# Handing the early expert jobs over to the late ones: two transposes ahead of outputs, one row load on another queue, scatters in a row, and the last gates in two halves

## Chip, cores and metric

The kernel runs on one core of one Trainium2 chip. The metric is the time on the device in microseconds (us) of one execution. A profiled execution is one more run, recorded by the hardware profiler; its span is the recorded stretch inside that execution.

## What is computed

The reference takes `x` of 8 x 512 tokens of width 256 and a context of 8 x 64 tokens, all float32, and does four steps in a row, each added to `x`:

```python
x = x + cross_attention_0(layernorm(x), ctx)          # 16 heads of 16
x = x + top_k_ffn(layernorm(x))                       # gelu on 384 of 512 tokens of each batch
x = x + cross_attention_1(layernorm(x), ctx, mask)
x = x + moe(layernorm(x))                             # 8 experts, top 2, inner width 1024

def moe(h):                                           # h: 4096 tokens x 256
    probs = softmax(h @ gate_w.T); w, idx = top_k(probs, 2); w = w / sum(w)
    for each expert e:
        g, u = split(h @ gate_up[e].T)
        out += combine[:, e] * ((silu(g) * u) @ down[e].T)
```

The last step is the larger half of the time. Here it is computed sparsely: each token goes through its two experts only.

## The kernel before, in words

**Front part.** For each batch a chain of steps does the two attentions, the first feed-forward, and then the routing (`route_steps`): the gate, the choice of two experts, and eight row scatters (`sent_off`, L864) on GpSimd (POOL), which write each token's normalised row, with its number and its two weights behind it, into the DRAM table `xs`, sorted by expert. The chains of the eight batches are interleaved by a string written out by hand, `ORDER`: a digit or letter stands for the next step of one chain, and `in_order` ties the instructions of every compute engine to that order. The last scatters of batch 7 are the last `7`s of the string. A scatter is also held until the matrix product that stands before it in the string is done (`products`).

**Early jobs.** A job is 256 rows of `xs` for one expert. Seven jobs (`NEARLY`) run inside the front part, chain `j`, on rows of batches 0 to 3. Each has: `load` (row number and expert from `jobs_early`, then the rows into `e_xg`), four `load_piece` and `load_down` (weights, on SyncE's queue), `enter` (four transposes `ps_e`, a copy to `e_xT` on ScalarE, and five small VectorE operations for token numbers and weights), four steps `gates(n)` of two chunks each (`gate_up`: four matmuls, a tanh on ScalarE, two VectorE operations, into `e_hT`), and two steps `down(k)` (eight matmuls, the weighted product `e_now` on VectorE, and an indirect DMA on POOL that adds the rows to the output, `add_rows`, L106). There is a single set of weights, `e_wgu` and `e_wdn`, and a single `e_sg`, so the tanh of a chunk waits until VectorE is done with the chunk before. PSUM tiles of this part come from `ps_m`, four buffers in turn.

**Lists.** `early_list` and `full_list` (chain `l`) work out on VectorE which expert and rows each job has. `full_list` stands behind job 6's `enter` in `ORDER`; it writes `jobs` and `job_e` for the late full jobs. `small_list` and `unit_list` are traced later and fill VectorE's gaps beside job 6's gates.

**Late jobs.** 18 full jobs of 256 rows (`NLATE`), seven of 128 rows and ten or eleven pairs of up to 64 rows run after the front part, in the list `order`; the last in it is a full job. Each has `load` (row numbers, rows into `xg`, weights into one of four sets, all on SyncE's queue), `enter` (transposes `ps_x`, copy to `xjT`), gates (`gate_up_full` or `gate_up_rows`) and `down`. The loop runs `down` of a job behind the gates of the next one. The first late job is special: its `load` was called with `late=True`, which puts its row load behind its gate weights, and its `enter` follows the last `down` of the early jobs. Row loads wait for `routed`, the scatters of batch 7. `unit_list` also writes rows of zeros behind each expert's rows (L1080, L1082, on POOL), after the row loads of the first two late jobs have landed; the pairs' row loads wait for that.

What `down` sends must wait for the adds of the job before it, since two jobs may hold the same token:

```python
ahead[:] = sent          # the adds of the job before
sent.clear()
...
sent.append(add_rows(now, tok[:, k : k + 1]))
```

Of the kernel before, what the change touches and what calls it, by code (L numbers as in the profile page):

```python
# [8 lines left out]
F32 = mybir.dt.float32  # L9
I32 = mybir.dt.int32  # L10
AF = mybir.ActivationFunctionType
ALU = mybir.AluOpType
# [3 lines left out]
P = 128  # L16
# [3 lines left out]
D = 256  # L20
H = 16
DK = 16
NC = D // P
# [4 lines left out]
E = 8  # L28
TOPK = 2
FF = 1024  # L30
NF = FF // P
# [3 lines left out]
QROWS = B * S + P  # L35
RW = D + 4
NFULL = 25
NEARLY = 7
NLATE = NFULL - NEARLY
# [15 lines left out]
5264345645256352452222F36F35F63F222246455635547335546357453674356647435356733333556646v7  # L55
l63333476G464jj77j5jGj666j5j7jj47Gjjj765j7457j4G5j64654j7j6556747j5j7644644444j76sH6jj56
4444j557j76j7j57jj7Hsj76jjjjHH7565j65jj676jj7jj6j57j5j6j75557j5555jj7j6j667j55557jjjs67j
66j76j7676j66j76s66667j7jjjj7jj6666j77j7j7jjjjj77jjs7j7j7j7j7j777jj77jjjljj77jj77jj
"""


# [1 line left out]
def xattn_ffn_kernel(ctx: ExitStack, tc: tile.TileContext, a: dict, out: bass.AP):  # L63
    nc = tc.nc
# [52 lines left out]
    with ExitStack() as front:  # L117
        const = front.enter_context(tc.tile_pool(name="const", bufs=1))
        work = front.enter_context(tc.tile_pool(name="work", bufs=2))
        small = front.enter_context(tc.tile_pool(name="small", bufs=4))  # L120
# [986 lines left out]
        e_xg = part_of_room(2, RW)  # L1107
        e_xT = part_of_room(NC, 2, P)
        e_sg = [part_of_room(1, 2 * P)]
        e_now = keep.tile([P, 2, D], F32, name="e_now")  # L1110
        e_w = {}
        piece = 2 * P

# [128 lines left out]
        chains["j"] = early = []  # L1242
        jobs_steps = [early_steps(j) for j in range(NEARLY)]
        early += jobs_steps[0][0]
        for j, (_, steps) in enumerate(jobs_steps):

            loads = list(jobs_steps[j + 1][0]) if j + 1 < NEARLY else []
            for n, step in enumerate(steps):
                early.append(step)
                if loads and n != len(steps) - 2:  # L1250
                    early.append(loads.pop(0))


        engines = (
# [46 lines left out]
    def kind(j):  # L1301
        return "full" if j < NLATE else "one" if j < NLATE + NONE else "pair"

    def load(j, late=False):

        what = kind(j)
        subs, n = (2 if what == "full" else 1), (2 if what == "pair" else 1)
        first = j if what != "pair" else NLATE + NONE + 2 * (j - NLATE - NONE)
        size = P if what != "pair" else P // 2

        with tc.issue_after(last.pop().ins) if last else nullcontext():
            at = [
                (
                    nc.sync.value_load(
                        jobs[0:1, 0, u : u + 1], min_val=0, max_val=E * QROWS + P - subs * size
                    ),
                    nc.sync.value_load(jobs[0:1, 1, u : u + 1], min_val=0, max_val=E - 1),
                )
                for u in range(first, first + n)
            ]  # L1320
        xg = moe.tile([P, 2, RW], F32, tag="xg", name=f"xg_{j}", bufs=3)

        def rows():
            for u, (row, _) in enumerate(at):
                i = nc.sync.dma_start(
                    xg[u * size : u * size + size, 0:subs, :],
                    xs[bass.ds(row, subs * size), :].rearrange("(s p) w -> p s w", p=size),
                ).ins

                if what == "pair":  # L1330
                    after(i, tail_sent)
                else:
                    for other in tail_sent:
                        tc.declare_no_dep(i, other, reason="rows of tokens alone")
                    after(i, routed)

        if not late:
            rows()
        w = []
        for u in range(n):  # L1340
            pool = wpool[sets[0] % 4]
            sets[0] += 1
            wgu = pool.tile([P, NC, 2 * FF], F32, tag="wgu", name=f"wgu_{j}_{u}")
            wdn = pool.tile([P, NF, D], F32, tag="wdn", name=f"wdn_{j}_{u}")
            w.append((wgu, wdn))
        for (_, e), (wgu, _) in zip(at, w):
            for c in range(NC):
                nc.sync.dma_start(
                    wgu[:, c, :], gu_t[bass.ds(e, 1), :, c, :].rearrange("e p o -> (e p) o")
                )  # L1350
        if late:
            rows()
        for (_, e), (_, wdn) in zip(at, w):
            i = nc.sync.dma_start(wdn, dn_t[bass.ds(e, 1), :, :, :].rearrange("e p f o -> (e p) f o"))
        last.append(i)
        return xg, w
# [127 lines left out]
    assert sorted(order) == [j for j in range(NJOB) if j != spare]  # L1484

    def load_at(i):
        return load(order[i], i == 0) if i < len(order) else None

    loads = [load_at(0), load_at(1)]
    entered = []  # L1490
    in_order(lambda: entered.append(enter(order[0], loads[0][0])))

    def placed(i, step):

        if i < NPIN:
            got = []
            in_order(lambda: got.append(step()))
            return got[0]
        return step()

    pending = None
    for i, j in enumerate(order):
        w = loads.pop(0)[1]
        xT, tok, wt = entered.pop(0)
        if i > 0:
            loads.append(load_at(i + 2))
        if i == 0:

            hT = placed(i, lambda: gate_up_full(j, xT, w, None, range(NF // 2)))
            entered.append(placed(i, lambda: enter(order[1], loads[0][0])))  # L1510
            placed(i, lambda: gate_up_full(j, xT, w, hT, range(NF // 2, NF)))
        elif j < NLATE:
            hT = placed(i, lambda: gate_up_full(j, xT, w))
        else:
# [67 lines left out]
```

## Time and profile before

| what | value |
|---|---|
| median of 3 runs | 1172.83 us (1172.62 to 1174.27) |
| the profiled execution's own time | 1164.97 us |
| its span | 1163.3 us |
| TensorE busy | 1144.1 us, 98% of the span |
| VectorE, ScalarE, GpSimd busy | 571.8, 375.7, 285.1 us |
| DMA | 203.53 MB, mean 175 GB/s |
| first matmul of the late jobs' gates | 574.59 us after the span's start |
| end of the last matmul | about 1155.8 us |

In the profile PE is TensorE, PEld its weight loads, DVE VectorE, ACT ScalarE, POOL GpSimd and SP SyncE; SPq and ACTq are DMA issues from those engines' queues. A row of a timeline gives start, duration, engine, source line, operation, output and input, and how many instructions are merged; in square brackets stands the idle time of that engine before the row, and what ended it. A float32 matmul of the code shows as two records. Where the row says `x_sb` as output or input of the early jobs, the tile is a part of that buffer (`e_xg`, `e_xT`, `e_sg`, `e_hT` lie in its first half, which is free by then).

### The profile page before, as it was taken

What the parts mean: (1) busy time and instruction counts of PE and PEld (TensorE: products, weight loads), DVE (VectorE), ACT (ScalarE), POOL (GpSimd) and SP (SyncE); (2) the same over time, 40 slices, a digit from 0 to 9 for tenths busy, and PEclk for the clock granted to TensorE, in tenths of its full rate; (3) what the DMA queues carried; (4) which work ended last, traced back from release to release, by engine and by line L of the source; (5) the groups of instructions that cost most, each with busy time, mean ns of one, the idle gap of its engine ahead of it and who ended that gap; (6) DMA issues with size and microseconds to landing.
All of it is one profiled execution on the core that took longest, in us unless ns stands there. A gap on an engine that the chain in (4) does not pass through costs nothing. (4 is left out here: it accounts for less than half of the span.)

```text
span 1163.3 us, 20921 instructions
## 1 busy us (share of the span) xinstructions
PE 1144.1 (98%) x8016; PEld 823.8 (71%) x8016; DVE 571.8 (49%) x1660; ACT 375.7 (32%) x717; POOL 285.1 (25%) x312
## 2 busy tenths in 40 slices
PE   8999999999999999999999999999999999999997
PEld 4556666656667778778887776777767777667886
DVE  6798888898877766555722221222222221222221
ACT  4655655645544342322222112121121211211210
POOL 6330134233340512332411212112121121211112
PEclk9999999999999999999999999999999999999999
DMA  9000001010134444355889689997798977986711
GB/s 271 3 1 2 1 20 39 19 57 20 38 119 137 128 128 134 108 160 156 265 331 341 218 282 300 322 307 226 265 310 312 315 235 269 307 313 228 277 15 19
DMA packets 119589, 203.53 MB, mean 175 GB/s; under 512 B 10401, under 2 KB 105249, under 8 KB 107969
## 3 DMA queue, kind: packets, MB, share of 16 engines
q1 hardware_dynamic: 100048, 179.35, 44.0%
q0 software_dynamic: 14640, 18.12, 7.7%
q10 hardware_dynamic: 4800, 4.72, 1.2%
q8 instruction: 64, 1.05, 0.4%
q14 instruction: 37, 0.30, 0.1%
HBM read 180.38 MB, written 23.47 MB: 175 GB/s over the span
## 5 line engine op out<-in xcount | busy, mean ns | idle before, releaser
L1397 PE MATMUL gu<-xjT,wgu 128*128 128x256 f32 x1152 | 252.0, 379 | 0.7 <-ACT xjT L1367 0.7
L1397 PEld LDWEIGHTS gu<-xjT,wgu 128*128 128x128 f32 x1152 | 217.6, 190 | 31.0 <-issue 1.2
L106 POOL DMA_INDIRECT out_dram<-now,tok x63 | 98.1, 1557 | 475.7 <-DVE now L1462 287.1
L1454 PE MATMUL o<-wdn,hT 128*128 128x256 f32 (+1 forms) x1008 | 189.2, 380 | 0.0
L1454 PEld LDWEIGHTS o<-wdn,hT 128*128 128x128 f32 (+1 forms) x1008 | 151.1, 173 | 28.3 <-issue 1.7
L1406 DVE TENSOR_TENSOR hT<-sg,gu 128x256 f32<-128x256 f32 x144 | 60.6, 421 | 189.4 <-ACT sg L1405 189.2
L1405 ACT ACTIVATE sg<-gu 128x256 f32<-128x256 f32 x144 | 55.3, 384 | 208.5 <-PE gu L1397 207.1
L1424 PE MATMUL gr<-wgu,xjT 128*64 128x512 f32 (+1 forms) x432 | 120.8, 596 | 0.0
L1183 PE MATMUL gu_e<-x_sb,e_wgu 128*128 128x256 f32 x448 | 101.6, 382 | 0.6 <-ACT x_sb L1162 0.6
L1183 PEld LDWEIGHTS gu_e<-x_sb,e_wgu 128*128 128x128 f32 x448 | 83.8, 190 | 15.6 <-issue 2.2
L1462 DVE TENSOR_SCALAR now<-o,wt 128x256 f32<-128x256 f32 x53 | 25.6, 483 | 139.1 <-PE o L1454 139.0
L1424 PEld LDWEIGHTS gr<-wgu,xjT 128*64 128x64 f32 (+1 forms) x432 | 42.8, 150 | 68.4 <-issue 66.9
L864 POOL DMA_INDIRECT xs<-xr,slots x64 | 63.2, 988 | 104.7 <-issue 35.4
L438 POOL TENSOR_TENSOR rstd<-ve,mhalf 128x4 f32<-128x4 f32 x32 | 33.0, 1030 | 223.3 <-DVE ve L436 177.8
L531 DVE TENSOR_REDUCE mx<-sc 128x32 f32<-128x2048 f32 x32 | 73.2, 2288 | 14.9 <-PE sc L524 14.6
L1434 DVE TENSOR_TENSOR h<-sg,gr 128x512 f32<-128x512 f32 x34 | 23.4, 688 | 82.9 <-PE gr L1424 82.8
L494 PE MATMUL ps_q<-xT,w_wq 128*128 128x512 f32 x128 | 62.0, 612 | 0.5 <-ACT xT L465 0.5
L1433 ACT ACTIVATE sg<-gr 128x512 f32<-128x512 f32 x34 | 20.3, 597 | 124.7 <-PE gr L1424 124.7
L625 PE MATMUL py<-w_wo,cT 128*128 128x256 f32 x256 | 60.3, 384 | 0.0
L625 PEld LDWEIGHTS py<-w_wo,cT 128*128 128x128 f32 x256 | 47.3, 190 | 11.6 <-issue 5.3
L447 ACT ACTIVATE xn<-x_sb,shift,rstd 128x256 f32<-128x256 f32 x96 | 49.8, 594 | 11.6 <-DVE shift L444 11.5
L433 DVE BATCH_NORM_STATS2 st<-x_sb 128x6 f32<-128x256 f32 x128 | 51.3, 400 | 3.6 <-DMA x_sb<-in_x_dram 3.6
(295 smaller groups left out, 1452.9 us busy)
## 6 DMA issues: line engine op xcount, KB each, us to landing
wgu<-in_guT_dram SPq DMA_DIRECT2D x90, 1024.0 KB, 9.7
wdn<-in_dnT_dram SPq DMA_DIRECT2D x45, 1024.0 KB, 6.0
e_wgu<-in_guT_dram SPq DMA_DIRECT2D x56, 256.0 KB, 3.6
e_wdn<-in_dnT_dram SPq DMA_DIRECT2D x7, 1024.0 KB, 6.0
xg<-xs SPq DMA_DIRECT2D x18, 260.0 KB, 7.2
out_dram<-x_sb ACTq DMA_DIRECT2D x8, 512.0 KB, 4.6
x_sb<-in_x_dram SPq DMA_DIRECT2D x7, 512.0 KB, 8.2
x_sb<-xs SPq DMA_DIRECT2D x7, 260.0 KB, 2.8
```

The costliest lines, as they stand in the source:

```text
L106: i = nc.gpsimd.indirect_dma_start(out=out_rows, out_offset=bass.IndirectOffsetOnAxis(ap=tok, axis=0), in_=rows, in_offset=None, bounds_ch ...
L433: nc.vector.bn_stats(st, x_sb[:, b * TB + t, :])
L494: nc.tensor.matmul(ps, lhsT=w["wq"][:, k, c * P : (c + 1) * P], rhs=got["xT"][:, k, :], start=(k == 0), stop=(k == NC - 1),)
L531: nc.vector.tensor_reduce(got["mx"].rearrange("p t (r h) -> p r t h", r=NQ)[:, :, :, 2 * c : 2 * c + 2], sc, AX.X, ALU.max,)
L625: nc.tensor.matmul(py[:, s, :], lhsT=cT[:, c, t * P : (t + 1) * P], rhs=w["wo"][:, c, :], start=(c == 0), stop=(c == NC - 1),)
L864: i = nc.gpsimd.indirect_dma_start(out=xs, out_offset=bass.IndirectOffsetOnAxis(ap=slots[:, t, k : k + 1], axis=0), in_=xr[:, t, :], in_of ...
L1183: nc.tensor.matmul(ps[:, half, :], lhsT=e_w["gu"][:, c, o : o + P], rhs=e_xT[:, c].rearrange("p s q -> p (s q)"), start=(c == 0), stop=(c ...
L1397: nc.tensor.matmul(ps[:, half, :], lhsT=wgu[:, c, o : o + P], rhs=xT[:, c].rearrange("p s q -> p (s q)"), start=(c == 0), stop=(c == NC - 1),)
L1405: nc.scalar.activation(sg[:, 0 : 2 * P], ps[:, 0, :], AF.Silu)
L1406: nc.vector.tensor_tensor(hT[:, f, :], sg[:, 0 : 2 * P], ps[:, 1, :], ALU.mult)
L1424: nc.tensor.matmul(ps[rows], lhsT=xT[:, c, 0, rows], rhs=wgu[:, c, o : o + 4 * P], start=(c == 0), stop=(c == NC - 1),)
L1454: nc.tensor.matmul(ps[rows], lhsT=hT[:, f, s * P + rows.start : s * P + rows.stop], rhs=wdn[:, f, :], start=(f == 0), stop=(f == NF - 1),)
```

## The change

1. `ORDER` and the chain `j`: job 6's `enter` stands ahead of the two `down` steps of job 5. The eight scatters of batch 7 stand closer together, all before the second `down` of job 5; before, they were spread among job 5's outputs and job 6's gates.
2. `first_rows`, `first_enter`: the first late job's rows are loaded into `e_xg` by an issue from ScalarE's queue, in the step of job 6's last two gate chunks. Its transposes, copy and small operations stand ahead of job 6's first `down`, in the front part, with a PSUM tile of `ps_m`; the result is `first_xT`, `first_tok`, `first_wt`. The first late job has no `xg` any more, and `load` loses its `late` form.
3. The last late job: four chunks of gates, then `down` of the job before, then the other four chunks, then its own `down`. Before, all eight chunks stood ahead of the `down` of the job before.

```diff
-66j76j7676j66j76s66667j7jjjj7jj6666j77j7j7jjjjj77jjs7j7j7j7j7j777jj77jjjljj77jj77jj
+66j76j7676j66j76s66667j7jjjj7jj6666j77j7j7jjjjj77jjs7j7j7j7j7j777j77j7777jjjljjjjj
...
+        first_xT = part_of_room(NC, 2, P)
         e_now = keep.tile([P, 2, D], F32, name="e_now")
+        first_tok = keep.tile([P, 2], I32, name="first_tok")
+        first_wt = keep.tile([P, 2], F32, name="first_wt")
+
+        def first_rows():
+            row = nc.scalar.value_load(
+                jobs[0:1, 0, 0:1], min_val=0, max_val=E * QROWS + P - 2 * P
+            )
+            i = nc.scalar.dma_start(
+                e_xg, xs[bass.ds(row, 2 * P), :].rearrange("(s p) w -> p s w", p=P)
+            ).ins
+            for other in tail_sent:
+                apart(i, [other], "rows of tokens alone")
+            after(i, routed)
+
+        def first_enter():
+            ps = ps_m.tile([P, NC, 2, P], F32, tag="m", name="ps_e_first")
+            for c in range(NC):
+                for k in range(2):
+                    nc.tensor.transpose(ps[:, c, k, :], e_xg[:, k, c * P : (c + 1) * P], ident)
+            nc.scalar.copy(first_xT, ps)
+            nc.vector.tensor_copy(first_tok, e_xg[:, :, D].bitcast(I32))
...
+            nc.vector.tensor_tensor(first_wt, first_wt, wt2, ALU.add)
...
-        for j, (_, steps) in enumerate(jobs_steps):
-            loads = list(jobs_steps[j + 1][0]) if j + 1 < NEARLY else []
+        for j, (_, steps) in enumerate(jobs_steps[:-1]):
+            loads, steps = list(jobs_steps[j + 1][0]), list(steps)
+            if j == NEARLY - 2:
+                steps.insert(-2, jobs_steps[-1][1].pop(0))
             for n, step in enumerate(steps):
                 early.append(step)
-                if loads and n != len(steps) - 2:
+                if loads and (n < NF // 2 + 1 or n == len(steps) - 1):
                     early.append(loads.pop(0))
+        steps = jobs_steps[-1][1]
+        early += steps[:-3] + [lambda: (first_rows(), steps[-3]())]
+        early += [lambda: (first_enter(), steps[-2]()), steps[-1]]
...
-    def load(j, late=False):
+    def load(j):
...
-        if not late:
-            rows()
...
-        if late:
-            rows()
...
-    in_order(lambda: entered.append(enter(order[0], loads[0][0])))
+    entered = [(first_xT, first_tok, first_wt)]
...
+        elif i == len(order) - 1 and j < NLATE:
+            hT = gate_up_full(j, xT, w, None, range(NF // 2))
+            down(*pending)
+            pending = None
+            gate_up_full(j, xT, w, hT, range(NF // 2, NF))
```

More of the change, by code (lines that the diff above doesn't have):

```diff
@@ L57 @@
 4444j557j76j7j57jj7Hsj76jjjjHH7565j65jj676jj7jj6j57j5j6j75557j5555jj7j6j667j55557jjjs67j
-66j76j7676j66j76s66667j7jjjj7jj6666j77j7j7jjjjj77jjs7j7j7j7j7j777jj77jjjljj77jj77jj
+66j76j7676j66j76s66667j7jjjj7jj6666j77j7j7jjjjj77jjs7j7j7j7j7j777j77j7777jjjljjjjjj
 """
@@ L1109, in xattn_ffn_kernel @@
         e_sg = [part_of_room(1, 2 * P)]
+        first_xT = part_of_room(NC, 2, P)
         e_now = keep.tile([P, 2, D], F32, name="e_now")
+        first_tok = keep.tile([P, 2], I32, name="first_tok")
[17 more added lines that the diff above has]
+            nc.vector.tensor_copy(first_tok, e_xg[:, :, D].bitcast(I32))
+            wt2 = small.tile([P, 2], F32, tag="wt2", name="wt2_first")
+            ej = job_e[:, 0:1]
+            nc.vector.scalar_tensor_tensor(
+                first_wt, e_xg[:, :, D + 1], ej, e_xg[:, :, D + 2], ALU.is_equal, ALU.mult
+            )
+            nc.vector.scalar_tensor_tensor(
+                wt2, e_xg[:, :, D + 1], ej, e_xg[:, :, D + 3], ALU.not_equal, ALU.mult
+            )
+            nc.vector.tensor_tensor(first_wt, first_wt, wt2, ALU.add)
         e_w = {}
@@ L1320, in load @@
             ]
[L1321 to L1335, printed above, removed]
-        if not late:
-            rows()
+        xg = moe.tile([P, 2, RW], F32, tag="xg", name=f"xg_{j}", bufs=3) if j > 0 else None
+        for u, (row, _) in enumerate(at) if j > 0 else []:
+            i = nc.sync.dma_start(
+                xg[u * size : u * size + size, 0:subs, :],
+                xs[bass.ds(row, subs * size), :].rearrange("(s p) w -> p s w", p=size),
+            ).ins
+            if what == "pair":
+                after(i, tail_sent)
+            else:
+                for other in tail_sent:
+                    tc.declare_no_dep(i, other, reason="rows of tokens alone")
+                after(i, routed)
         w = []
@@ L1486, in load_at @@
     def load_at(i):
-        return load(order[i], i == 0) if i < len(order) else None
+        return load(order[i]) if i < len(order) else None
     loads = [load_at(0), load_at(1)]
-    entered = []
-    in_order(lambda: entered.append(enter(order[0], loads[0][0])))
+    entered = [(first_xT, first_tok, first_wt)]
     def placed(i, step):
```

## The prediction

> **What bounds the kernel now.** First the page's busy shares: TensorE is at 98%, so only its idle time and its tail can be won.
>
> ```profile
> PE 1144.1 (98%) x8016; PEld 823.8 (71%) x8016; DVE 571.8 (49%) x1660; ACT 375.7 (32%) x717; POOL 285.1 (25%) x312
> ```
>
> Second, the waits of TensorE. They are short everywhere; three lie where the early jobs hand over to the late ones, 1.6 us together.
>
> ```profile
> PE gu L1397 <- ACT xjT L1367: 0.7, 1, 0.7
> PE gu_e L1183 <- ACT x_sb L1162: 0.6, 1, 0.6
> PE ps_x L1365 <- DMA xg<-xs: 0.3, 1, 0.3
> ```
>
> Third, TensorE's timeline there. An undisturbed 32 gate records take 7.07 us (L1210 at 543.26), so one matmul of the code (two records) takes 0.432 us and a chunk of four 1.73 us. Early job 6's L1210 takes 7.43: 0.36 us of hidden stall.
>
> ```profile
> 543.26 7.07 PE L1210 MATMUL o_e<-e_wdn,x_sb 128*128 128x256 f32 x32
> 550.16 0.60 PE L1159 MATMUL ps_e<-ident,x_sb 128*128 128x128 f32 x4
> 551.49 14.22 PE L1183 MATMUL gu_e<-x_sb,e_wgu 128*128 128x256 f32 x64 [0.61 <-ACT x_sb L1162]
> 565.55 7.43 PE L1210 MATMUL o_e<-e_wdn,x_sb 128*128 128x256 f32 x32
> 573.29 0.63 PE L1365 MATMUL ps_x<-ident,xg 128*128 128x128 f32 x4 [0.31 <-DMA xg<-xs]
> 574.59 7.17 PE L1397 MATMUL gu<-xjT,wgu 128*128 128x256 f32 x32 [0.68 <-ACT xjT L1367]
> ```
>
> Fourth, busy time by stretch (PE, PEld, DVE, ACT, POOL, each with its instructions, then granted clock, DMA share and GB/s): from 560 to 570 VectorE is full, because the job lists (full, small, unit) share it with job 6's gates.
>
> ```profile
> 560.00:570.00 10.00, 9.91 (x46) 8.41 (x45) 9.79 (x49) 2.28 (x6) 3.30 (x4) 1.00 0.75 265
> ```
>
> So ScalarE's tanh of each chunk waits for VectorE and runs behind TensorE: the tanh of chunk 5 comes at 564.29, though TensorE finished that chunk near 561.9.
>
> ```profile
> 564.29 0.39 ACT L1191 ACTIVATE x_sb<-gu_e 128x256 f32<-128x256 f32 x1 [1.00 <-DVE r_b_o L1028]
> 565.69 0.39 ACT L1191 ACTIVATE x_sb<-gu_e 128x256 f32<-128x256 f32 x1 [1.01 <-DVE x_sb L1193]
> ```
>
> Fifth, SyncE's timeline: job 0's gate weights go out at 559.09, its rows at 570.19, `wdn` behind them.
>
> ```profile
> 559.09 0.91 SPq L1348 DMA_DIRECT2D wgu<-in_guT_dram  x2
> 570.19 0.39 SPq L1325 DMA_DIRECT2D xg<-xs  x1
> 570.78 0.38 SPq L1354 DMA_DIRECT2D wdn<-in_dnT_dram  x1
> ```
>
> Last, the tail on POOL: the last add starts 0.28 us after its product (`now`, 1155.86 + 0.48).
>
> ```profile
> 1154.32 1.56 POOL L106 DMA_INDIRECT out_dram<-now,tok  x1 [3.04 <-DMA out_dram<-now,tok]
> 1156.62 1.55 POOL L106 DMA_INDIRECT out_dram<-now,tok  x1 [0.75 <-DVE now L1462]
> ```
>
> **Part 1, job 6's transposes ahead of job 5's outputs.** The four transposes still cost TensorE 0.44 us (550.16 to 550.60), now before L1210, and the 0.61 us wait goes, since the copy has two outputs (6.9 us) to hide under. The products would then be followed by `pn_f` and the gates at 550.75 instead of 551.49. But chunk 4 needs the PSUM buffer of chunk 0, which VectorE frees only after `full_list`, at 558.48 now, when TensorE is there at 558.4 already (14.22 us instead of 13.98 shows the touch). VectorE's list starts with `cnt_f`, at 551.53; without the five small operations of `enter` in front (they move ahead of the first product) it starts right behind the second product, about 551.22. So VectorE's chain, and with it everything to the end of the gates, gains 0.3 us, not 0.7: the gates end at 565.55 - 0.3 = 565.24.
>
> **Part 2, the scatters closer.** Batch 7's eight scatters run in a row on POOL: from 549.43 at 1.29 us each the last starts at 558.5 instead of 567.75 and, landing 3.0 to 3.6 us after issue, is in by 562. Behind them the two adds of job 5 move from 552.1 and 556.6 to about 559.8 and 561.7; they land by 569, before job 6's products need `e_now`. Cost nothing; without that cover, the delay of those landings.
>
> **Part 3, first rows by ScalarE's queue.** In the changed program's order the load of the row number and the issue stand on ScalarE between the tanh of chunk 5 and that of chunk 6. All they wait for is in by 562, so the place decides: tanh 5 ends at 564.29 + 0.39 - 0.3 = 564.38. The trace has no register load on ScalarE. SyncE takes 1.38 us from the end of `wdn`'s issue (571.16) to the next issue (572.54) with two such loads between; half is 0.7, bounds 0.35 and 1.4. I take 0.7: issue at 565.1. The tanhs of chunks 6 and 7 queue behind it, and VectorE behind them; tanh 6 came at 565.69 before, so at about 565.5 it is not late, and at the upper bound 0.5 us late, under the stall that follows.
>
> **Part 4, its transposes ahead of job 6's outputs.** TensorE comes to them at 565.24, with the rows issued at 565.1. Behind them in TensorE's strict order stand all of job 6's outputs, which need no rows. That is a new stall: the landing time. The same 260 KB from `xs` took 2.7 to 2.8 us in four of the seven early loads, with a quiet queue; that is the lower bound. But now `wdn` of job 0 follows its gate weights at once, then job 1's rows and weights, so from 560 on the DMA engines are full. What fullness costs: ScalarE's own 512 KB store took 4.6 us at the median and 5.8 at 530.75 with the DMA share at 0.85 (+1.1); row scatters took 3.0 and, beside full weight loads at 579 to 584, 5.7 (+2.7). So 3.9 to 5.5 us, and 5.8 as the end; I take 4.2, nearer the ScalarE row because queue and kind are the same. Rows in at T = 569.3 (567.4 to 571.6 over both bounds).
>
> [...]
>
> After T: transposes 0.44, sixteen products 6.91, drain 0.17. Then job 0's first gate starts, and here stands a second new wait: its PSUM bank is that of job 6's last output, so TensorE waits for VectorE's read (0.04 + 0.48 + 0.05 by the row at 573.02, which the transposes used to cover). It starts at T + 8.14. Before: 574.59. The change breaks even at T = 566.45; at 569.3 it loses 2.85 us. In this sum the removed 0.31, 0.68 and 0.36 are already counted.
>
> **Part 5, last gates parted.** The same matmuls in another order. Chunk 7's `hT` is ready about 1.0 us after its matmuls (ScalarE 0.38, VectorE 0.42, hand-overs); the outputs need it at their eighth matmul, 3.0 us later, so no stall. Job 16's adds go out 6.9 us earlier and the add at 1154.32 loses its wait, but POOL was free again at 1155.88 and the last add waited for its product, not for that. Zero; at best a few tenths if its landing shares engines less, which the DMA slices (idle between the two) do not suggest.
>
> From 576 on TensorE is busy without a break, as before; rows of the pairs (issued 588.96, used at 602.76) come some microseconds earlier or no later than TensorE.
>
> **Sum.** The profiled execution took 1164.97 us (span 1163.3): +2.85 gives 1167.8. The runs' median is 1172.83, 7.9 above; taking that offset as common, 1175.7.
>
> **Rivals.** (a) *The rows land in time: not slower.* Everything hangs on T. With the load at 0.35 us and a landing of 2.7, T is 567.4 and the loss 1.0 us; if, further, ScalarE's chain ran 1 us or more ahead of my reading, T falls under 566.45 and the change wins, at most down to T = 565.24, which is 1.2 us. For it: four landings of 2.8. Against: full DMA engines and VectorE's 9.79 of 10. It decides from T = 566.45. Time 1171.6 to 1174.0.
>
> (b) *TensorE's clock drops in the stall.* At the end the granted clock is 1.00 until 1160.00 and 0.58 on average to 1163.30. A drop to zero would lie at 1161.9, so the drop came between 4.2 and 6.1 us after the last matmul (1155.83). My stall is 4.1 us. If it drops, and comes back as late as it went, the loss is (1 - 0.58) of 4.2 to 6.1 us: 1.8 to 2.6 more, 1177.5 to 1178.3, and 1179 with a late landing. Against: the stall is just under the time seen.
>
> [...]
>
> (c) *Part 1 gains nothing.* If VectorE's chain does not start its 0.3 us earlier, ScalarE's issue and T come 0.3 us later as well and the loss is 3.15 us, 1176.0. It lies inside the main case, and I give it 0.1 of the chances there.
>
> **Numbers.** Main case, (c) in it (T 567.9 to 571, +1.5 to +4.5): 0.58. (a): 0.22. (b): 0.20. What a measurement of this kernel can tell from no change is about 0.2%, 2.3 us. Slower by more: T above 568.8, some 0.7 of main, and all of (b): 0.6. Faster by more would need 2.3 us, beyond the best case's 1.2, save for an error of mine: 0.05. The rest, 0.35, is same. Range: from 1172.4, inside (a), to 1178.8, the end of (b), since run to run 1.7 us was seen.
>
> **What would show it.** Right: in the changed profile TensorE waits 3 to 5 us at `ps_e_first` for the DMA of `xs` issued by ScalarE near 565; the 0.61 and 0.68 us waits are gone; 0.5 us of wait for `e_now` before job 0's first gate; `wdn` of job 0 near 561 on SyncE; POOL's scatters in one row ending near 559.5; the last add still follows its product. Wrong: no wait at `ps_e_first`, or an issue before 563 or after 567, or a granted clock under 1 there.

## The result and the profile after

The changed kernel takes 1185.82 us (median of 5 runs, 1184.45 to 1187.4), the kernel before beside it 1173.7 us (1172.62 to 1175.29). The ratio is 1.0105, 95% interval 1.0092 to 1.0119: 12.1 us slower, where the forecast was 2.9 us slower and the range ended 6 us over before. The direction and the place were right, the size was not. The profiled execution took 1184.45 us, its span 1182.7. All ratios in this document are of fast runs; one run of 5976 us, of the kernel without the first rows, is left out of them as slow.

**Busy shares.** TensorE has the same matmuls and 5.3 us more busy time than in before's profile. That is a trap: the kernel before, profiled again where it takes 1174 us, has 1149.5 too (below). The page's shares do not show the loss; the waits do.

```profile
PE 1149.4 (97%) x8016; PEld 827.3 (70%) x8016; DVE 571.7 (48%) x1660; ACT 374.7 (32%) x717; POOL 285.4 (24%) x312
```

**TensorE's waits.** The three short waits at the hand-over are gone. In their place stands one of 10.1 us, for the rows that ScalarE loads, the longest of the kernel, and one of 0.73 us ahead of job 0's first gate.

```profile
PE ps_e_first L1131 <- DMA x_sb<-xs: 10.1, 1, 10.1
```

**TensorE's timeline** (start, length, line, output and inputs, number of records, then the idle time before and what ended it). Read the stretch from the end of job 5's gates (549.89, where before had 543.26) to job 0's first gate (594.12, before 574.59).

```profile
549.89 0.60 PE L1191 MATMUL ps_e<-ident,x_sb 128*128 128x128 f32 x4
...
583.83 1.08 PE L1131 MATMUL ps_e_first<-ident,x_sb 128*128 128x128 f32 x4 [10.11 <-DMA x_sb<-xs]
584.71 8.68 PE L1242 MATMUL o_e<-e_wdn,x_sb 128*128 128x256 f32 x32
594.12 7.14 PE L1429 MATMUL gu<-x_sb,wgu 128*128 128x256 f32 x32 [0.73 <-issue]
```

The stretch was 31.33 us and is 44.23, 12.90 more. Four terms make it up. The row of job 6's gates ends 23.83 us after its start instead of 22.45 (551.49 + 14.22): +1.38. The stall: +10.11. The transposes take 0.88 us instead of 0.44 and the outputs 8.68 instead of 7.07: +2.05. What is left behind the gates, without stall and at full speed, is 8.24 us instead of 8.88: -0.64, the removed waits (0.36, 0.31 and 0.68) less the new one of 0.73. From job 0's first gate to the end of the span it is 588.6 us, before 588.7: nothing is given or won later.

**Granted clock** (the third number from the end; before it the busy times of PE, PEld, DVE, ACT and POOL in each stretch, behind it the DMA share and GB/s). TensorE stops at 573.7; the granted clock falls from 1.00 to 0.50 at about 577.7 and comes back only at 588, four microseconds after the work (583.83). The slow outputs are these.

```profile
578.00:580.00 2.00, 0.00 (x0) 0.00 (x0) 0.00 (x0) 0.00 (x0) 0.00 (x0) 0.50 1.13 368
584.00:586.00 2.00, 2.00 (x8) 1.73 (x8) 1.97 (x13) 0.59 (x1) 1.29 (x2) 0.50 0.98 378
588.00:590.00 2.00, 2.00 (x11) 1.74 (x11) 0.02 (x1) 0.00 (x0) 0.00 (x0) 1.00 0.48 164
```

**ScalarE and SyncE.** ScalarE issues the row load 0.96 us after tanh 5 ends (573.16 + 0.38); the rows land 9.3 us after the issue. Ahead of it SyncE has issued job 0's gate weights and `wdn` (3 MB), job 1's rows (0.26 MB) and job 1's gate weights (2 MB). In the kernel before only the 2 MB of job 0's gate weights were ahead of the first rows.

```profile
573.16 0.38 ACT L1223 ACTIVATE x_sb<-gu_e 128x256 f32<-128x256 f32 x1 [1.00 <-DVE r_b_o L1028]
574.50 0.41 ACTq L1120 DMA_DIRECT2D x_sb<-xs  x1
```

```profile
568.85 1.43 SPq L1382 DMA_DIRECT2D wgu<-in_guT_dram  x2
570.34 0.38 SPq L1386 DMA_DIRECT2D wdn<-in_dnT_dram  x1
...
572.98 1.69 SPq L1382 DMA_DIRECT2D wgu<-in_guT_dram  x2
```

**The queues, packet by packet.** The DMA view of a short window says how many packets of each queue were moved (packets, MB, share of the 16 engines). q1 is SyncE's queue, q10 ScalarE's, q0 POOL's. The rows are 272 packets of about 1 KB; `wdn` moves in 1 KB packets too, the gate weights in 8 KB packets. The three views below are of 576 to 578, 578 to 580 and 580 to 583.5 us of the changed kernel.

```profile
q1 hardware_dynamic: 714, 0.73, 103.1%
```

```profile
q1 hardware_dynamic: 448, 0.50, 76.0%
q10 hardware_dynamic: 234, 0.23, 36.6%
```

```profile
q1 hardware_dynamic: 279, 1.42, 100.6%
q10 hardware_dynamic: 38, 0.03, 2.9%
```

So the landing has three parts. Until 578.2, 3.7 us after the issue, not one packet of ScalarE's queue is moved. Then 234 of the 272 go in 1.8 us, beside 373 of SyncE's, most of them of 1 KB; from 579 to 579.5 it is 78 beside 88. The last 38 take 3.3 us, at a time when SyncE's packets become the 8 KB ones of job 1's gate weights. Those packets are the likely reason (two later profiles of the same kernel without them lack this part), but 38 against 279 is far from like numbers, and what else slowed these 38 is open.

### The profile page after: what moved, and what is told of

Same layout as the page of the kernel before. It is cut to its first block, busy times and chain, and to the rows that moved or that the text cites. A ratio compares the mean times of both kernels' runs of the same rounds, so it can differ in the third digit from the quotient of the medians.

```text
span 1182.7 us, 20935 instructions
## 1 busy us (share of the span) xinstructions
PE 1149.4 (97%) x8016; PEld 827.3 (70%) x8016; DVE 571.7 (48%) x1660; ACT 374.7 (32%) x717; POOL 285.4 (24%) x312
## 5 line engine op out<-in xcount | busy, mean ns | idle before, releaser
L1429 PE MATMUL gu<-xjT,wgu 128*128 128x256 f32 x1088 | 238.1, 379 | 0.0
L1429 PEld LDWEIGHTS gu<-xjT,wgu 128*128 128x128 f32 x1088 | 205.6, 190 | 28.5 <-issue 1.2
L106 POOL DMA_INDIRECT out_dram<-now,tok x61 | 95.2, 1561 | 450.5 <-DVE now L1494 302.8
```

Source lines behind the costliest of these rows:

```text
L106: i = nc.gpsimd.indirect_dma_start(out=out_rows, out_offset=bass.IndirectOffsetOnAxis(ap=tok, axis=0), in_=rows, in_offset=None, bounds_ch ...
L1429: nc.tensor.matmul(ps[:, half, :], lhsT=wgu[:, c, o : o + P], rhs=xT[:, c].rearrange("p s q -> p (s q)"), start=(c == 0), stop=(c == NC - 1),)
```

## The experiments

Two theories of the landing went into them. *First in, first out*: the rows come after all that SyncE issued before them, at the 0.365 MB per us that the engines move (the view above has 368 GB/s from 578 to 580; 5.26 MB from 569.3 on end at 583.7, the very time). *Turns*: the queues share the engines, whatever came first. Others asked what the stall does to the clock, and what the other parts of the change are worth. Times are given as ratios to the kernel before in the same group of runs. There were several groups, and before took 1166 us in some and 1172 to 1174 in others, with no overlap. What makes this difference is not shown: the record gives chip number 4 to a group of either kind, 37 minutes apart.

**The kernel before, again**, with no edit.

> The kernel before, unchanged, to see how much of the 6.6 us by which the changed kernel's profile is already late at the products of job 5 (549.89 against 543.26) belongs to the kernel at all: the program is the same up to there, so nothing of it should. Expected: job 5's products start nearer 550 than 543 in this profile, and the stretch from them to job 0's first gate is again 31.3 us within 0.5.

> The kernel before, unchanged, on the chip of the runs below. Where the changed kernel and its variants ran on the chip with the longer times, VectorE stood still for 0.4 to 0.8 us three times in job 6's gates and SyncE issued job 0's weights 4.5 us after the lists. If those belong to that chip and not to the change, this profile shows them too when this chip is a slow one (1172 us or more), and not when it is a fast one (1166 us).

Job 5's outputs start here, in the first and in the second of these profiles:

```profile
544.22 7.07 PE L1210 MATMUL o_e<-e_wdn,x_sb 128*128 128x256 f32 x32
```

```profile
552.17 7.07 PE L1210 MATMUL o_e<-e_wdn,x_sb 128*128 128x256 f32 x32
```

The first took 1165.65 us in a group where before has a median of 1166.18, the second 1173.94 where it has 1172.46. The same program comes to this place 8 us apart, and takes 31.32 and 31.48 us from there to job 0's first gate. So the 6.6 us by which the changed kernel's first profile is late at 549.89 come with the group of runs, not with the change (the first control missed its expectation of 550; the second shows why). The profile of before that the prediction read was of the quicker kind, though its timed runs were of the slower. The second has no standstill of VectorE, SyncE issues 1.4 us after the lists, and its TensorE is busy for 1149.5 us.

**Without the first rows.** The rows of job 0 are loaded by SyncE behind its gate weights and transposed behind job 6's outputs, as before; the moved transposes of job 6, the scatters and the parted gates stay.

```diff
-        early += steps[:-3] + [lambda: (first_rows(), steps[-3]())]
-        early += [lambda: (first_enter(), steps[-2]()), steps[-1]]
+        early += steps
...
+        if late:
+            rows()
...
+    in_order(lambda: entered.append(enter(order[0], loads[0][0])))
```

> Of the change only the transposes of job 6 ahead of job 5's outputs, the scatters in a row and the parted last gates; job 0's rows come by SyncE behind its gate weights and are transposed behind job 6's outputs, as before. If the whole loss comes from the first rows (ScalarE's load and its early transposes), this kernel takes the time of the kernel before or up to 0.5 us less (0.9995 to 1.000). If the scatters or the transposes of job 6 carry part of the loss (job 6's gates were 1.6 us longer after the change), it is 1 to 2 us slower (1.001 to 1.002).

> The kernel without the first rows' parts, again. If before takes about 1172 us here: should VectorE stand still in job 6's gates and SyncE issue job 0's weights 4.5 us after the lists in this kernel too, then those come with the closer scatters or the moved transposes and cost it 1 to 1.5 us (ratio 1.001); if not, they come with the first rows, and the ratio is again 0.999.

> The kernel without the first rows' parts. If before takes about 1172 us here: with the standstill (SyncE's first issue 4.5 us after the lists, job 6's gates 15 us or more) it comes with the closer scatters or the moved transposes, ratio 1.000 to 1.002; without it, with the first rows, ratio 0.999 again. If before takes about 1166 us: 0.999, and the question stays open.

Ratios 0.9991 (0.9982 to 1.0), 0.9989 (0.9980 to 0.9998) and 0.9994 (0.9984 to 1.0003). Without the first rows nothing of the loss is left, in three groups where before takes 1166 us (the changed kernel itself loses 6.3 us in such a group, below); the rest of the change is worth about 1 us there. In the second profile job 6's outputs start 22.44 us after the start of the stretch (565.91 against 543.47), 0.15 us later than in before, and what follows is quicker:

```profile
573.03 0.60 PE L1371 MATMUL ps_x<-ident,xg 128*128 128x128 f32 x4
```

The 0.31 us wait for the rows is gone: with the scatters in a row, SyncE issues job 0's rows at 565.08 and not at 570.19. The stretch is 30.84 us, half a microsecond shorter; where the other half of the gain lies was not found.

**SyncE's later loads held until the rows are in.** Only job 0's gate weights stay ahead.

```diff
+            first_load.append(i)          # in first_rows, the row load
...
+            if j == 0:
+                after(i.ins, first_load)  # i: the load of wdn
```

> The changed kernel, but SyncE's load of job 0's wdn, and with it all that SyncE issues behind it, waits until the first rows have landed. So only job 0's gate weights (2 MB) are ahead of the rows instead of 5.3 MB. Theory 'first in, first out' (the rows land after all that SyncE issued before them, at 0.365 MB per us): the landing falls from 9.3 us to 3 us or less, the clock stays up, and the kernel is 8 to 10 us faster than the changed one (ratio to before about 1.002). Theory 'turns' (the rows share the engines with whatever is in flight, whatever their place): less in flight helps as well, landing 3 to 4 us; so this run shows that the backlog makes the 9.3 us, not yet how. Theory 'the row load is slow in itself' (indirect address, ScalarE's queue): landing stays at 6 us or more and the time hardly moves.

Ratio 1.0034 (1.0021 to 1.0048). The landing is 3.5 us at most, where the changed kernel has 6.4 in a group of the same kind (below) and 9.3 in the first profile: the backlog made it, not the load itself. Between 569 and 570 the rows have the engines nearly alone, and 263 of the 272 packets go in that microsecond; the first came 1.8 us after the issue. The profile puts the end of the stall down to VectorE's last operation on job 6's gates, done 0.1 us before it, so the rows may have landed a little earlier.

```profile
q10 hardware_dynamic: 263, 0.26, 79.6%
```

But TensorE's granted clock still dropped, to 0.50, in a stall of 3.44 us, and the outputs took 9.62 us. What "the clock stays up" got wrong is what the prediction got wrong too.

```profile
570.58 1.09 PE L1133 MATMUL ps_e_first<-ident,x_sb 128*128 128x128 f32 x4 [3.44 <-DVE x_sb L1227]
571.45 9.62 PE L1244 MATMUL o_e<-e_wdn,x_sb 128*128 128x256 f32 x32
```

**The first rows on SyncE's queue, ahead of job 0's weights.**

```diff
-            row = nc.scalar.value_load(
+            row = nc.sync.value_load(
...
-            i = nc.scalar.dma_start(
+            i = nc.sync.dma_start(
```

> The changed kernel, but the first rows are issued by SyncE, ahead of job 0's gate weights, instead of by ScalarE. Then nothing of job 0 is ahead of them. They wait for the lists and the scatters alone, are issued near 566 on the changed kernel's clock and land 3 to 4 us later, before TensorE comes to them at 573.7: no stall, no clock drop. If the loss is the backlog, the time is that of the kernel before or 0.5 to 1.5 us less (ratio 0.999 to 1.000); job 0's gate weights come 0.5 to 1 us later, which should be free as they are used 15 us later. If the early transposes themselves cost (PSUM bank, ScalarE's copy), it stays 1 us or more slower.

> The first rows by SyncE ahead of job 0's weights, again. Where before takes 1166 us it was level (0.9995). If the standstill comes with the first rows, it shows here as well, SyncE's rows go out 3 us later and land about when TensorE comes to them: ratio 1.000 to 1.002. If not, 0.999 to 1.000.

> The first rows by SyncE ahead of job 0's weights. If before takes about 1172 us here and the standstill shows, SyncE issues the rows 3 us later and they land about when TensorE comes to them: ratio 1.000 to 1.002. Without it 0.999. If before takes about 1166 us: 0.999, and the question stays open.

Ratios 0.9995 (0.9986 to 1.0004), 0.9990 (0.9980 to 0.9999) and 0.9992 (0.9983 to 1.0001): level or some tenths to 1 us quicker. Two things differ from the changed kernel at once, the queue and the place: by SyncE the rows go out 18.0 us after the start of the stretch, by ScalarE 22.4 (last profile of the changed kernel, below). Second profile: the rows go out at 562.35, ahead of the weights, and TensorE finds them there.

```profile
562.35 0.38 SPq L1120 DMA_DIRECT2D x_sb<-xs  x1
```

```profile
566.82 0.60 PE L1131 MATMUL ps_e_first<-ident,x_sb 128*128 128x128 f32 x4
...
575.06 7.14 PE L1429 MATMUL gu<-x_sb,wgu 128*128 128x256 f32 x32 [0.73 <-issue]
```

From the transposes to job 0's first gate it is 8.24 us (the prediction said 8.14). The early transposes cost nothing that these times show; only the wait for their rows did.

**The changed kernel, again**, with no edit.

> The changed kernel, unchanged, beside the variants and on their chip. Two things of its first profile are open: job 6's gates took 15.66 us there (14.5 in the three variants run so far) and SyncE's first weight load was issued 4.5 us after the job list was written (about 1.5 in the variants). If these belong to the change, they come again and the loss is again 12 us (ratio 1.010). If they do not, SyncE's weights go out near 560.4 and ScalarE's row load near 567, and what is left is the stall: by 'first in, first out' 5.3 MB are ahead of the rows, landing near 575, stall 8 us, ratio 1.008 to 1.010; by 'turns' (landing 4 us) stall 4 us, ratio 1.003 to 1.005.

> The changed kernel, unchanged, beside the kernel before on the same chip. If the standstill of VectorE and SyncE's late issue are the chip's, both kernels show them or neither does. On a chip without them SyncE's first weights go out 8 us earlier against TensorE, so more of the backlog is gone when ScalarE issues the rows: stall 6 to 9 us instead of 10, ratio 1.005 to 1.009; on a chip with them stall 10 us, ratio 1.008 to 1.011.

> The changed kernel, unchanged, as the reference of this chip: 9 to 13 us over before, with a stall of 7 to 10 us at the first transposes.

Ratios 1.0076 (1.0052 to 1.0100) and 1.0108 (1.0087 to 1.0128) where before takes 1172 to 1173 us, and 1.0054 (1.0039 to 1.0070) where it takes 1166.5. The stalls are 10.0, 7.4 and 6.2 us, the landings 9.2, 6.6 and 6.4; the second expectation had 10 us for its stall, and the third 9 to 13 us of loss where it is 6.3. In the last two all the rows are in before SyncE's 8 KB packets come, so the 3.3 us of the last packets are missing; the wait for the first packet is not. The stall of the last of them, and its view of 569 to 571, the rows issued at 565.50:

```profile
571.92 1.09 PE L1131 MATMUL ps_e_first<-ident,x_sb 128*128 128x128 f32 x4 [6.21 <-DMA x_sb<-xs]
```

```profile
q1 hardware_dynamic: 484, 0.50, 70.6%
q10 hardware_dynamic: 269, 0.26, 37.9%
```

The expectations speak of a standstill: VectorE idle in the middle of job 6's gates, and SyncE's first weights late. They tied it to the change or to the chip. It goes with neither alone: it stands in all seven profiles of kernels with ScalarE's row load in the groups where before takes 1172 us or more, in none of the three in the others, and in neither profile without the first rows in the slower groups (before, and the parted gates alone). With one exception (1.43 us, ended by ScalarE) VectorE's long gaps there end on nothing but its own last instruction, 0.3 to 1.0 us each.

```profile
568.89 0.22 DVE L928 TENSOR_TENSOR ml_o<-ones_e,j_o 128x56 f32<-128x56 f32 x1 [0.80 <-DVE x_sb L1225]
```

The two variants that could have told whether it comes with the first rows ran three times, each time where before takes 1166 us. Its cause stays open; its size is 0.6 to 1.4 us of job 6's gates, and weights that SyncE issues 3 us later.

**The later loads issued just behind the rows** instead of being held until they land.

```diff
+                if j == NEARLY - 1 and f == NF - 2:
+                    first_load.append(t)  # t: the tanh of chunk 6
...
+            if j == 0:
+                after(i.ins, first_load)  # i: the load of wdn
```

> The changed kernel, but SyncE's load of job 0's wdn and all it issues later wait for ScalarE's tanh of chunk 6, the instruction right behind the row load's issue. So the same 5.3 MB are issued, 2 MB ahead of the rows (and nearly in by then) and the rest just behind them, instead of all ahead. 'First in, first out': the rows land as when wdn was held until they were in (3.5 us), stall 3.4 to 4 us, ratio 1.003 to 1.005. 'Turns' or any other sharing with what comes behind: the landing is 5 us or more, stall over 5 us, ratio 1.006 to 1.010.

Ratio 1.0056 (1.0037 to 1.0075), landing 3.5 us, stall 4.29. The landing is the one of *first in, first out*; stall and ratio lie just above its range (3.4 to 4 us, 1.003 to 1.005) and below the other's. The packets say that it is right for another reason: the first one came 1.6 us after the issue, and from 575 to 576 the rows had the engines almost to themselves because `wdn` had only begun (here too VectorE's last operation on the gates was done just before the stall ended):

```profile
q10 hardware_dynamic: 238, 0.24, 73.0%
q1 hardware_dynamic: 38, 0.05, 16.1%
```

**The row load one step earlier.**

```diff
-        early += steps[:-3] + [lambda: (first_rows(), steps[-3]())]
+        early += steps[:-4] + [lambda: (first_rows(), steps[-4]()), steps[-3]]
```

> The changed kernel, but ScalarE issues the row load one step (2.8 us) earlier, ahead of the tanh of chunk 4, so near 564.1 instead of 567. Ahead of the rows are then job 0's gate weights and wdn and job 1's rows, 3.3 MB, but not job 1's gate weights (2 MB, issued from about 564.8). 'First in, first out': 3.3 MB at 0.365 MB per us from 560.8 on are in at 569.8, and the rows land then: landing 5.7 us, stall 2.7 to 3.2 us, ratio 1.002 to 1.004. 'Turns': landing 4 us, rows in at 568, stall 1 us, ratio 1.000 to 1.001. If the place in the queue does not matter, the rows land as late as in the changed kernel.

Ratio 1.0069 (1.0045 to 1.0094), stall 5.4 us, landing 7.8 us: longer than either theory said.

```profile
579.67 1.08 PE L1131 MATMUL ps_e_first<-ident,x_sb 128*128 128x128 f32 x4 [5.38 <-DMA x_sb<-xs]
```

The first packet came 3.6 us after the issue, into the 8 KB packets of job 0's gate weights. From 575.5 to 577 the queues moved packets in like numbers, 58 to 42, so the rows got 0.04 MB while SyncE got 0.48:

```profile
q1 hardware_dynamic: 58, 0.48, 78.3%
...
q10 hardware_dynamic: 42, 0.04, 8.2%
```

That is what *first in, first out* cannot give: rows moving while the whole of `wdn`, issued ahead of them, still waits (SyncE's 0.48 MB are the 8 KB packets of the gate weights).

**Only job 1's gate weights held back**, until the tanh behind the rows' issue.

```diff
+                if j == 1:
+                    after(g.ins, first_load)  # g: a load of wgu; first_load as above
```

> The changed kernel, but only job 1's gate weights (2 MB, the ones that move in 8 KB packets) and what SyncE issues after them wait for ScalarE's tanh of chunk 6, the instruction behind the row load's issue. Job 0's weights and job 1's rows stay ahead of the rows. 'First in, first out' in bytes: 3.3 MB are ahead instead of 5.3, all in 9.4 us after SyncE's first issue, so the landing falls to 4 us. 'Turns, a packet at a time': the rows' packets start as late as in the changed kernel (3.6 us after issue) and then share with job 0's wdn (1 KB packets) as there, but the last tenth no longer waits behind 8 KB packets (3.3 us in the changed kernel): landing 5.5 to 6.5 us, stall 6.5 to 7.5 us, ratio 1.005 to 1.008. If the packets start 1.5 to 2 us after issue, as when SyncE had issued nothing for 4 us, what holds the first packet is SyncE's issues and not the traffic, and the landing is 4 to 5 us.

Ratio 1.0079 (1.0057 to 1.0101), landing 9.6 us: both theories missed. SyncE issued the held weights 0.9 us after the rows, but the rows' first packet came only 3.7 us after their issue. They had 1 us beside the 1 KB packets of `wdn`; from 581.5 on the 8 KB packets came. From 582 to 585 only 106 of the rows' packets went between them:

```profile
q1 hardware_dynamic: 206, 1.14, 94.3%
q10 hardware_dynamic: 106, 0.10, 10.1%
```

So what comes behind matters too, and the wait for the first packet decides which it meets. That wait was 1.6 and 1.8 us in the two kernels where SyncE had nothing but job 0's gate weights out, and 3.6 to 3.8 us in all eight profiles where it had issued `wdn` as well, whether 0.2 us before the rows or 5.5. What holds the packet back was not found.

**The first transposes behind job 6's outputs.**

```diff
-        early += [lambda: (first_enter(), steps[-2]()), steps[-1]]
+        early += [steps[-2], lambda: (steps[-1](), first_enter())]
```

> The changed kernel, but the first rows are transposed behind job 6's outputs, as in the kernel before (ScalarE still loads them). TensorE comes to them 7 us later, near 574. If the loss is the wait for the rows and the clock lost in it, the stall shrinks by 7 us (8 becomes 1 to 1.5, 10 becomes 3), job 0's first gate waits 0.7 us more for ScalarE's copy, and the ratio is 1.000 to 1.003, with the clock at 1 throughout if the stall is under 2.5 us. If transposing early costs in itself, the ratio stays above 1.005.

Ratio 1.003 (1.0009 to 1.0052). With the same late rows the stall at the first transposes is 2.1 us instead of 10: the place in TensorE's order is what made the landing dear. The clock did not hold at 1 even so; the 2.5 us of the expectation was the author's estimate, and no run shows such a limit:

```profile
586.61 0.66 PE L1131 MATMUL ps_e_first<-ident,x_sb 128*128 128x128 f32 x4 [2.13 <-DMA x_sb<-xs]
```

```profile
586.00:588.00 2.00, 0.67 (x5) 0.47 (x5) 0.58 (x4) 0.58 (x1) 0.63 (x1) 1.00 1.01 351
588.00:590.00 2.00, 2.00 (x5) 1.64 (x6) 0.00 (x0) 0.00 (x0) 1.50 (x2) 0.53 1.09 347
```

After two gaps, 2.13 and 0.72 us with 0.66 us of transposes between, it is down from 588.1 on. The ten runs lie between 1171.67 and 1181.28 us with granted clocks of 0.999 to 0.992 in the same order; the profile shows one of the long ones (1180.04).

**TensorE kept busy through the stall.** Sixteen needless matmuls ahead of the first transposes.

```diff
+            for n in range(16):
+                nc.tensor.matmul(
+                    ps[:, 0].rearrange("p k q -> p (k q)"),
+                    lhsT=ident,
+                    rhs=e_xT[:, 0].rearrange("p s q -> p (s q)"),
+                    start=True,
+                    stop=True,
+                )
```

> The changed kernel with 16 needless matmuls (6.9 us) on TensorE between job 6's gates and the first transposes, written into the PSUM tile that the transposes overwrite; they lie in the wait for the rows. If the dropped clock costs what the profiles show (job 6's outputs 8.7 us instead of 7.07, transposes 0.88 instead of 0.44, so 2.0 us), the clock stays at 1.00, the outputs take 7.07 us and the kernel is 2 us faster than the changed one (ratio to it 0.998). If the long outputs have another cause (traffic, PSUM), they stay at 8.5 us or more and the time is the changed kernel's.

The mechanism is as expected: the clock stays at 1.00, the transposes take 0.44 us from start to start and the outputs 7.07. The stretch is 37.60 us (544.30 to 581.90) where the changed kernel in the same group has 39.61: 2.0 us less.

```profile
574.00:576.00 2.00, 2.00 (x12) 1.79 (x11) 1.95 (x14) 0.59 (x1) 0.10 (x1) 1.00 1.00 413
```

```profile
574.10 7.07 PE L1250 MATMUL o_e<-e_wdn,x_sb 128*128 128x256 f32 x32
581.90 7.14 PE L1437 MATMUL gu<-x_sb,wgu 128*128 128x256 f32 x32 [0.73 <-issue]
```

The medians differ by less, 1172.29 against 1172.84 us, four runs each, and the intervals of their ratios to before overlap (1.0033 to 1.0063 and 1.0039 to 1.0070). So the 2.0 us are shown in the stretch, not in the time of the whole kernel.

**The parted gates alone**, in the kernel before.

```diff
+        elif i == len(order) - 1 and j < NLATE:
+            hT = gate_up_full(j, xT, w, None, range(NF // 2))
+            down(*pending)
+            pending = None
+            gate_up_full(j, xT, w, hT, range(NF // 2, NF))
```

> The kernel before with the last gates parted (the outputs of job 16 between the two halves of job 17's gates) and nothing else. Predicted at zero: ratio 0.999 to 1.001, the last add still right behind its product; the end of the changed kernel's first profile came 0.1 us sooner after the last matmul. If parting moves the last add, the ratio leaves that interval.

Ratio 1.0000 (0.9989 to 1.0010): nothing, as forecast.

## Why the prediction was right or wrong, step by step

**Part 1 (0.3 us gained).** Wrong by little, and as rival (c) had it: in nine profiles with the moved transposes, all where before takes 1166 us, the row of job 6's gates ends 22.58 to 22.63 us after the stretch begins, in before 22.45. VectorE's chain did not start earlier: `cnt_f` comes 8.46 us after the start in the last profile of the changed kernel, 8.27 in before. Most of the half microsecond that the change gains without the first rows comes from Part 2, which was priced at zero: the scatters in a row let SyncE issue job 0's rows 5 us earlier, which takes the 0.31 us wait away.

**Part 2 (no cost).** The scatters run as forecast: one row on POOL, the last at 565.18, 15.3 us after the stretch begins as forecast, the two adds behind it. Whether the standstill comes with them is open.

**Part 3 (load of the row number 0.7 us).** Measured 0.96 us from the end of tanh 5 to the issue. In the quicker groups the issue is 22.4 us after the start of the stretch (565.50 against 543.12), forecast 21.84.

**Part 4, the step that failed: the landing.** Forecast 4.2 us with 2.7 and 5.8 as ends; measured 9.3 in the first profile, and 6.4, 6.6 and 9.2 in the others of the same kernel. What failed is the price of a full machine, read from rows that did not have this backlog. The store at 530.75 had met engines as full as here (DMA share 1.03 from 530 to 536; the 0.85 is the mean to 540), but SyncE moved 2.5 MB in the 15 us around it. Here it had issued 5.3 MB ahead of the rows, since the change itself removed what held those loads back. The prediction named that (`wdn` follows at once, then job 1's loads) and still priced it as the fullness of before. And before had nearer rows: the other three of its seven early loads of 260 KB landed in 5.6, 6.2 and 9.0 us, and the same load in the late full jobs, behind weights on SyncE's own queue, took 7.2 us at the median.

```profile
xg<-xs SPq DMA_DIRECT2D x18, 260.0 KB, 7.2
```

In two views in which both queues are busy, their packets go in like numbers: from 569.5 to 570.5 in the last profile of the changed kernel the rows have 182 packets and SyncE 188, all of about 1 KB, and in the kernel with the earlier issue 42 and 58 from 575.5 to 577, when SyncE's are of 8 KB. In two others they do not: 38 against 279 in the first profile of the changed kernel, 106 against 206 where only job 1's gate weights were held back. The forecast of 4.2 us had a term neither for packets of unequal size nor for the wait for the first packet, 3.7 us in the first profile.

**After T: 8.14 us.** Measured 8.24 with the clock up (573.66 to 581.90 with the needless matmuls, 566.82 to 575.06 with SyncE's rows). The wait ahead of job 0's first gate was 0.73 us instead of 0.57 (the profile names nothing that ended it; VectorE's read of the bank ends 0.21 us before the gate). This term was right.

**Rival (b), the clock.** Priced at 1.8 to 2.6 us and given one chance in five, because the prediction's stall of 4.1 us lay just under the 4.2 to 6.1 us seen at the kernel's end. It happened in all nine profiles with a stall of 2.1 us or more that was not filled, and cost 2.05 us in the first. The drop came 2.7 to 5.4 us after the last matmul, in two kernels after the work had come back, so a stall under 4.2 us was no safety (it dropped in a stall of 3.44 us, and in one of 2.13 with a gap of 0.72 close behind). Read in steps of a quarter of a microsecond, the granted clock stays low for 3.41 us in three of the nine profiles, for 6.83 in three and for 10.24 in three: one, two and three times 3.41. What sets these lengths is not shown.

**Part 5 and what follows job 0's first gate (zero).** Right: ratio 1.0000, and the last add still waits for its product.

```profile
1176.12 1.56 POOL L106 DMA_INDIRECT out_dram<-now,tok  x1 [1.89 <-DVE now L1494]
```

**The sum.** Forecast: -0.3 + 4.1 - 0.9 = 2.9 us. Measured in the stretch: +1.4 (gates; 0.15 of it where VectorE does not stand still), +10.1 (stall), +2.05 (clock), -0.6 (removed waits less the new one; -0.8 counted as the forecast counts, from the next matmul's start) = 12.9. The standstill was in no view of before. The offset of 7.9 us between the profiled execution and the median is the distance between the two kinds of groups: the profile came from one of the quicker kind, the timed runs from the slower. Where before takes 1166 us the loss is 6.3 us, and this too is above the 6 us at which the range ended.

**A version without the loss.** Taking the first rows off ScalarE's queue, and issuing them behind or ahead of the weights on SyncE's, is enough. Without them the kernel is at 0.9989 to 0.9994 of before, with SyncE's load ahead of the weights at 0.9990 to 0.9995: about 1 us, in three comparisons each, of which one each has an interval wholly below 1. Both ran only where before takes 1166 us.

## What to carry to other kernels

Before a load is moved to a second queue, write down what the first queue will have in flight at that moment, in bytes and in packet sizes: here a second queue was no way past them (5.3 MB were ahead, and the rows' first packet came 3.7 us after the issue, the last 9.3). And where a strict order puts a transfer's first use ahead of work that does not need it, the transfer's worst landing is what counts (here 9.3 us, where four of the seven loads of the kernel before took 2.7 to 2.8), plus what the drop of the granted clock in the idle time costs (here 2.05 us). Issuing the small load first on the same queue cost nothing here, in three comparisons.

## What the runs showed that was not expected

- The rows' first packet was moved 1.6 to 1.8 us after the issue while SyncE had only gate weights out, and 3.6 to 3.8 us after it in every profile where SyncE had also issued `wdn`, whatever the packets then under way. The cause is open.
- 8 KB packets against 1 KB packets, 58 to 42 in number: 0.48 MB to 0.04 MB in 1.5 us.
- The granted clock fell after gaps of 2.13 and 0.72 us, came back 3.4 to 6.0 us after the work, and stayed low for 3.41, 6.83 or 10.24 us and nothing between.
- The same program takes 1166 us in some groups of runs and 1172 to 1174 in others, and the 8 us lie in the front part; the cause is open.
